# Queries, keys and values of the second layer from seven products of quarters instead of eight, in jobs of half a group

## The chip, the cores and the metric

The kernel runs on one core of one Trainium2 chip. The metric is the device time of one execution in microseconds (us), lower is better. TensorE (PE) multiplies matrices into PSUM; VectorE (DVE), ScalarE (ACT) and GpSimd (POOL) work on vectors; SyncE (SP) issues most of the transfers. Each engine runs its own instructions in the order of the program.

## What is computed

A graph attention layer (first layer) is followed by a self-attention layer (second layer), for 8 batches of 512 tokens with 512 features. All data is float32. Only the second layer is touched by the change:

```python
h = _sln(hidden, w, ...)                       # layer norm, scaled and shifted by the condition
qkv = (h @ Wqkv.T + bqkv).reshape(B, N, num_heads, hd, 3)     # 16 heads of 32
energy = jnp.einsum('bhqd,bhkd->bhqk', q, k)
att = jax.nn.softmax(energy, axis=-1) / D ** 0.5
out = jnp.einsum('bhqk,bhkd->bhqd', att, v)
out = jnp.moveaxis(out, 1, 2).reshape(B, N, D)
out = out @ Wp.T + bp
h1 = out + hidden
h2 = _sln(h1, w, ...)
return h2 + h1
```

## The kernel before

The first layer fills the first third of the span and writes its result to `mid` in DRAM. The second layer then goes through 128 steps, 16 for each batch b (`steps`, L683). A step is one group g of 4 heads and one block c of 128 queries; in this text a step is called by its place `at` (0 to 15) in its batch. All instructions are written out by hand in one loop (`tc.manual_schedule()`, at the end of the function), so each engine's order is the order in the text.

In step n the loop issues, in this order:

- in even steps, `weigh(n-2)` and `weigh(n-1)`: probabilities by values, into PSUM tile `pao` (PE, L731). In the last batch each step weighs one step instead;
- `scores(n+1)`: queries by keys for 4 heads into two PSUM tiles `s` of two banks each (PE, L694), and `tops(n+1)`: the maxima over each pair of heads (DVE, L700). There are just two such tiles, so the next scores wait until the exponentials have read these;
- `turn_probs(n, 0)` and `(n, 1)`: four PE transposes of a head's probabilities into one of 3 PSUM banks (`bank`, pool `ps_g`), and an ACT copy to SBUF (L718, L720);
- `exps(n+1)`: four exponentials on ACT (L706);
- the first half of a group: a group is one 128x512 block of q, k, v or of the output projection, 4 k-blocks added up in one of those 3 banks (class `Group`, L136). Each fp32 matmul is two PE instructions in the trace, so half a group is 4 instructions of 128x512;
- `normalize(n+1, 0)`: a reciprocal on DVE (L711) and two POOL multiplications (L713);
- `turn_probs(n, 2)` and `(n, 3)`, copied by DVE; `normalize(n+1, 1)`; the rest of an output block where one is due (`finish`, L652 to L655: two DVE instructions, one on POOL, one transfer);
- the second half of the group, and what empties it: an ACT activation with bias (q, k), an ACT copy (v), or for the projection a DVE addition to the residual (L644) and the statistics of the norm (L93 to L97);
- smaller items: norm statistics and norm of batch b+2 (L93, L111; steps 11 to 15), the turning of batch b+1 (`turn`, L123/L124: 4 PE transposes and one ACT activation each; steps 0 and 1, for batch 1 steps 0 to 3), the fetch of batch b+2, a bias on POOL (L115).

`group_of` says which group goes with which step: each step of a batch has exactly one. While batch b is attended to, 12 groups make q, k and v (most of them for batch b+1) and 4 project batch b-1. In the last batch, steps 0 and 1 make its last q and k, and 14 half groups of projections (`endings`) go with the other steps; `finish_last` (L656 to L681) makes the last output block with half-width (256-column) matmuls.

Of the kernel before, what the change touches and what calls it, by code (L numbers as in the profile page):

```python
# [9 lines left out]
F32 = mybir.dt.float32  # L10
# [9 lines left out]
P = 128  # L20
C = N // P
# [23 lines left out]
def graph_then_self_attention(ctx: ExitStack, tc: tile.TileContext, x, x_t, near, near_t, labels, w_self_t, wq, wk_t,  # L45
# [30 lines left out]
    feat = ctx.enter_context(tc.tile_pool(name="feat", bufs=3))  # L76
# [11 lines left out]
    XQ, Z, HT, Q, K, V, AO, GATE, STATS = {}, {}, {}, {}, {}, {}, {}, {}, {}  # L88
# [28 lines left out]
    def turn(b, f):  # L117

        if f == 0:
            HT[b] = feat.tile([P, C, N], F32, tag="feat", name=f"ht_{b}")  # L120
        pz = bank(f"pz_{b}_{f}")
        for c in range(C):
            nc.tensor.transpose(pz[:, c * P:(c + 1) * P], Z[b][:, c, f * P:(f + 1) * P], ident)  # L123
        nc.scalar.activation(HT[b][:, f, :], pz, AF.Identity, bias=gates_t[:, 1, f, b:b + 1], scale=gates_t[:, 0, f, b:b + 1])  # L124

    class Group:
# [5 lines left out]
        def half(self, n, take=True):  # L132
            if n == 0:
                self.out = bank(self.name)
            for k in (2 * n, 2 * n + 1):
                nc.tensor.matmul(self.out, self.stationary(k), self.moving(k), start=(k == 0), stop=(k == C - 1))  # L136
            if n == 1 and take:
                self.after(self.out)

    def q_or_k(b, i, f):  # L140
        def after(out):
            at = (HG * b + f) % 5
            dst = (qkp if at else qk0).tile([P, N], F32, tag=f"{'qk'[i]}{at}", name=f"{'qk'[i]}_{b}_{f}")
            nc.scalar.activation(dst, out, AF.Identity, bias=col["b_q" if i == 0 else "b_k"][:, f:f + 1])
            (Q, K)[i][b, f] = dst
        return Group(f"pqk_{b}_{i}_{f}", lambda k: W1[i][:, k, f * P:(f + 1) * P], lambda k: HT[b][:, k, :], after)

    def value(b, c):
        def after(out):
            if c == 0:  # L150
                V[b] = kv.tile([P, C, HM], F32, tag="kv", name=f"v_{b}")[:, :, 0:F]
            nc.scalar.copy(V[b][:, c, :], out)
        return Group(f"pv1_{b}_{c}", lambda k: HT[b][:, k, c * P:(c + 1) * P], lambda k: W1[2][:, k, :], after)


    with ExitStack() as l0:
# [3 lines left out]
        pro = l0.enter_context(tc.tile_pool(name="pro", bufs=1))  # L160
        ps = l0.enter_context(tc.tile_pool(name="ps0", bufs=4, space=PSUM))
# [3 lines left out]
        def bank(name):  # L165
            return ps.tile([P, 512], F32, tag="bank", name=name)
# [113 lines left out]
        def self_feat_main(b, blocks_of_f):  # L280
            if 0 in blocks_of_f:
                SF[b] = feat.tile([P, C, N], F32, tag="feat", name=f"sf_{b}")
            psf = {f: bank(f"psf_{b}_{f}") for f in blocks_of_f}
            for k in range(C):
                for f in blocks_of_f:
                    nc.tensor.matmul(psf[f], ws[:, k, f * P:(f + 1) * P], VT[b][:, k, :], start=(k == 0), stop=(k == C - 1))  # L286
            return psf
# [258 lines left out]
        for n, (b, c) in enumerate(slots):  # L546
# [18 lines left out]
            for i in {26: (0,), 27: (1,), 29: (2,), 30: (3,)}.get(n, ()):  # L565
                group = q_or_k(0, i, 0) if i < 2 else value(0, i - 2)
                group.half(0)
                group.half(1)
# [50 lines left out]
    qkp = ctx.enter_context(tc.tile_pool(name="qkp", bufs=1, reuse_waits="tile"))  # L619
    aop = ctx.enter_context(tc.tile_pool(name="aop", bufs=8, reuse_waits="tile"))  # L620
    gp = ctx.enter_context(tc.tile_pool(name="gp", bufs=2, reuse_waits="tile"))
# [3 lines left out]
    ps_g = ctx.enter_context(tc.tile_pool(name="ps_g1", bufs=3, space=PSUM))  # L625
# [5 lines left out]

    wp = W1[3]
# [3 lines left out]
    bv = w1.tile([P, C], F32, name="bv")  # L636

    def project(b, c):
        def after(out):
            if c == 0:  # L640
                GATE[b] = gp.tile([P, 2, F], F32, tag="gate", name=f"gate_{b}")
                nc.sync.dma_start(GATE[b], gates[b].partition_broadcast(P))
            h1 = XQ[b][:, c, :]
            nc.vector.tensor_tensor(h1, out, h1, ALU.add)  # L644
            statistics(h1, f"h1_{b}_{c}")
        return Group(f"ppj_{b}_{c}", lambda k: AO[b, k][:, c * P:(c + 1) * P], lambda k: wp[:, k, :], after)
# [49 lines left out]
    def tops(n):  # L696
        TOP[n] = small.tile([P, 4], F32, tag="top", name=f"top_{n}")
        DEN[n] = small.tile([P, 4], F32, tag="den", name=f"den_{n}")
        for pair in range(2):
            nc.vector.tensor_reduce(TOP[n][:, 2 * pair:2 * pair + 2], S[n][pair], AX.X, ALU.max, negate=True)  # L700

    def exps(n):
        E[n] = []
        for j in range(4):
            e = ep.tile([P, N], F32, tag="e", name=f"e_{n}_{j}")
            nc.scalar.activation(e, S[n][j // 2][:, j % 2, :], AF.Exp, bias=TOP[n][:, j:j + 1], accum_out=DEN[n][:, j:j + 1])  # L706
            E[n].append(e)
# [7 lines left out]
    def turn_probs(n, j):  # L715
        pt = bank(f"pt1_{n}_{j}")
        for k in range(C):
            nc.tensor.transpose(pt[:, k * P:(k + 1) * P], E[n][j][:, k * P:(k + 1) * P], ident)  # L718
        et = ET[n, j] = tp.tile([P, C, P], F32, tag="et", name=f"et_{n}_{j}")
        (nc.scalar.copy if j < 2 else nc.vector.tensor_copy)(et, pt.rearrange("p (k n) -> p k n", k=C))  # L720

    def weigh(n):
# [10 lines left out]
        if c == (0 if last else C - 1):  # L733
            AO[b, g] = aop.tile([P, N], F32, tag="ao", name=f"ao_{b}_{g}")
# [5 lines left out]
    def group_of(b, at):  # L740

        own = {0: (0, 1), 1: (1, 1), 2: (0, 2), 3: (1, 2), 4: (0, 3), 5: (1, 3)} if b == 0 else {0: (0, 3), 1: (1, 3)}
        if at in own:
            return q_or_k(b, *own[at])
        if b == B - 1:
            return None
        if b > 0 and at in (2, 4, 6, 8):
            return project(b - 1, at // 2 - 1)
        i = at - 6 if b == 0 or at > 8 else (at - 3) // 2
        if i in (2, 3, 4, 5):  # L750
            return value(b + 1, i - 2)
        return q_or_k(b + 1, i % 2, i // 2 if i < 2 else i // 2 - 2)


    endings = [(B - 2, 0), (B - 2, 1), (B - 2, 2), (B - 1, 0), (B - 1, 1), (B - 2, 3), (B - 1, 2)]
    ending = [project(*e) for e in endings]

    with tc.manual_schedule():
        nc.vector.tensor_scalar(bv, col["b_v"], att_scale, None, ALU.mult)
        nc.sync.dma_start(bp_bc, rows[ROW_BP].partition_broadcast(P))  # L760
        fetch(2)
        scores(0)
        tops(0)
        exps(0)
        for c in (2, 3):
            group = value(0, c)
            group.half(0)
            group.half(1)
        for pair in range(2):
            normalize(0, pair)  # L770

        for n, (b, g, c) in enumerate(steps):
            at = n % 16
            group = group_of(b, at)
            more = n + 1 < len(steps)
            if b == B - 1 and at > 0:
                if at > 1:
                    weigh(n - 2)
            elif n > 0 and n % 2 == 0:
                weigh(n - 2)  # L780
                weigh(n - 1)
            if more:
                scores(n + 1)
                tops(n + 1)
            for j in (0, 1):
                turn_probs(n, j)
            if more:
                exps(n + 1)
            if group:
                group.half(0)  # L790
            elif b == B - 1 and more:
                ending[at // 2 - 1].half(at % 2, take=False)
            if more:
                normalize(n + 1, 0)
            for j in (2, 3):
                turn_probs(n, j)
            if more:
                normalize(n + 1, 1)
            if 0 < b < B - 1 and at in (3, 5, 7, 9):
                finish(b - 1, (at - 3) // 2)  # L800
            if b == B - 1 and at > 2 and at % 2 and more:
                ending[at // 2 - 1].after(ending[at // 2 - 1].out)
            if b == B - 1 and at >= 4 and at % 2 == 0:
                finish(*endings[at // 2 - 2])
            if group:
                group.half(1)

            if 11 <= at < 16 and b + 2 < B:
                if at > 11:
                    norm(b + 2, at - 12)  # L810
                if at < 15:
                    norm_stats(b + 2, at - 11)
            if at < (4 if b == 0 else 2) and b + 1 < B:
                for f in (at,) if b == 0 else (2 * at, 2 * at + 1):
                    turn(b + 1, f)
            if at == 9 and b > 0 and b + 2 < B:
                fetch(b + 2)
            first = 0 if b == B - 1 else 10
            if first <= at < first + C:
                bias(b, at - first)  # L820
        ending[-1].half(1)
        weigh(len(steps) - 2)
        weigh(len(steps) - 1)
        finish(*endings[-1])
# [57 lines left out]
```

## Time and profile before

| | |
|---|---|
| runs | 1360.03, 1360.10, 1361.98 us; median 1360.1 us |
| the profiled execution | 1364.07 us, of which 1362.3 us are the span of the trace |
| granted TensorE clock | 0.996 |
| busy, share of the span | PE 99%, DVE 67%, ACT 50%, POOL 51% |
| scores of step 0 of batches 1 to 7 start at | 529.00, 648.32, 767.64, 886.96, 1006.28, 1125.60, 1244.92 us: 119.32 us a batch |
| within a batch, scores to scores | 6.41 us, 8.29 us where `weigh` lies between, alternating; with the turning of the next batch 7.28 and 9.16 |
| last batch | 5.70 to 6.16 us a step from its third step on |

A timeline row gives the start, the length, the engine, the line, the operation with its tiles and how many instructions are merged. A group row gives the line, engine, tiles, shape and count, then the busy time and the mean length of one, and the idle time in front of them with what ended it. PE's matmuls overlap: a row of a matmul is longer than the distance to the next one's start, so distances between starts are used below.

### The profile page before, as it was taken

How to read it: one execution, taken by the hardware profiler on the slowest of the kernel's cores; microseconds unless marked ns; L12 is line 12 of the kernel's file. 1: busy time of each engine (PE TensorE's matmuls, PEld its weight loads, DVE VectorE, ACT ScalarE, POOL GpSimd, SP SyncE). 2: the span in 40 equal slices, each digit the busy share in tenths (PEclk: the TensorE clock that was granted, in tenths of full speed). 3: DMA queues.
4: the chain of work that ended last, by engine and by line, in shares of the span. 5: the costliest groups of instructions: out<-in, count | busy, mean ns of one | idle time of the engine just before them, and what ended most of it. 6: DMA issues, size and time to landing. Idle time of an engine off the chain costs nothing.

```text
span 1362.3 us, 27708 instructions
## 1 busy us (share of the span) xinstructions
PE 1344.2 (99%) x10499; PEld 823.7 (60%) x10499; DVE 907.2 (67%) x1589; ACT 687.5 (50%) x1639; POOL 692.2 (51%) x808
## 2 busy tenths in 40 slices
PE   9999999999989999999999999999999999999997
PEld 6566666666665555555555555555555555555665
DVE  4567677677644556676576667657666765765797
ACT  1322223122225666656665665666566566656664
POOL 0255654465653345455455545545554554554665
PEclk9999999999999999999999999999999999999999
DMA  9614452262221000001001000100100010000010
GB/s 339 205 70 146 138 182 88 92 216 71 88 70 55 2 1 1 9 17 55 1 18 63 2 9 17 55 1 17 63 1 9 17 56 1 17 32 1 9 41 32
DMA packets 46514, 78.53 MB, mean 58 GB/s; under 512 B 9872, under 2 KB 14416, under 8 KB 46384
## 3 DMA queue, kind: packets, MB, share of 16 engines
q1 hardware_dynamic: 45440, 75.57, 16.1%
q8 instruction: 85, 1.39, 0.4%
q0 software_dynamic: 512, 0.66, 0.2%
q10 hardware_dynamic: 432, 0.55, 0.1%
q14 instruction: 45, 0.37, 0.1%
HBM read 59.27 MB, written 17.49 MB: 56 GB/s over the span
## 4 chain that ended last, share of the span: by engine, by line
PE 93%; DVE 4%; POOL 2%; issue 0%; DMA 0%; ACT 0%; POOLq 0%; DVEq 0%; ACTq 0%
PE pt L718 18%; PE pqk L136 16%; PE s L694 10%; PE pao L731 9%; PE pss L457 8%; PE ppj L136 8%; PE pv L136 8%; PE psf L286 7%; PE po L498 2%; PE pw L426 1%; PE ptw L486 1%; PE pz L123 1%; PE pq L407 1%; PE po L496 1%; POOL t L464 1%; POOL t L463 1%
## 5 line engine op out<-in xcount | busy, mean ns | idle before, releaser
L713 POOL TENSOR_SCALAR e<-e,den 128x512 f32<-128x512 f32 x512 | 374.0, 730 | 433.6 <-DVE den L711 383.0
L700 DVE TENSOR_REDUCE top<-s 128x2 f32<-128x1024 f32 x256 | 301.3, 1218 | 196.3 <-PE s L694 196.3
L706 ACT ACTIVATE e<-s,top 128x512 f32<-128x512 f32 x512 | 346.6, 700 | 16.9 <-DVE top L700 16.8
L718 PEld LDWEIGHTS pt<-ident,e 128*128 128x128 f32 x2048 | 229.4, 141 | 165.2 <-issue 89.8
L718 PE MATMUL pt<-ident,e 128*128 128x128 f32 x2048 | 273.1, 276 | 1.0 <-POOL e L713 0.9
L720 ACT COPY et<-pt 128x512 f32<-128x512 f32 x256 | 137.7, 589 | 223.5 <-PE pt L718 223.4
L136 PE MATMUL pqk<-ht,w 128*128 128x512 f32 x512 | 240.6, 593 | 0.0
L720 DVE COPY et<-pt 128x512 f32<-128x512 f32 x256 | 164.2, 683 | 0.9 <-PE pt L718 0.6
L694 PE MATMUL s<-k,q 32*128 32x512 f32 x1024 | 149.8, 641 | 0.0
L457 PE MATMUL pss<-kq,sf 128*128 128x320 f32 x512 | 143.2, 433 | 1.0 <-DVE kq L414 1.0
L731 PEld LDWEIGHTS pao<-et,v 128*32 128x32 f32 x4096 | 107.4, 110 | 42.2 <-issue 41.4
L731 PE MATMUL pao<-et,v 128*32 128x128 f32 x4096 | 126.7, 274 | 0.5 <-ACT ao L736 0.5
L136 PEld LDWEIGHTS pqk<-ht,w 128*128 128x128 f32 x512 | 87.6, 190 | 62.5 <-issue 62.1
L136 PE MATMUL pv<-w,ht 128*128 128x512 f32 x256 | 121.4, 600 | 2.1 <-DVE x L499 2.1
L457 PEld LDWEIGHTS pss<-kq,sf 128*128 128x128 f32 x512 | 94.9, 190 | 37.5 <-ACT sf L293 1.5
L136 PE MATMUL ppj<-w,ao 128*128 128x512 f32 x248 | 116.7, 593 | 0.0
L286 PE MATMUL psf<-vt,ws 128*128 128x512 f32 x256 | 115.0, 592 | 0.0
L706 ACT ACTIVATION_READ_ACCUMULATOR e<-s,top 128x1 f32 x512 | 111.2, 217 | 0.0
L711 DVE RECIPROCAL den<-den 128x2 f32<-128x2 f32 x256 | 42.5, 166 | 85.9 <-ACT e L706 85.9
L480 POOL TENSOR_TENSOR t<-t,den 128x640 f32<-128x640 f32 x32 | 40.7, 1272 | 83.4 <-DVE den L479 82.7
L286 PEld LDWEIGHTS psf<-vt,ws 128*128 128x128 f32 x256 | 48.3, 190 | 50.7 <-issue 46.6
L488 ACT COPY wt<-ptw 128x640 f32<-128x640 f32 x32 | 22.2, 693 | 108.0 <-PE ptw L486 107.6
(197 smaller groups left out, 1375.4 us busy)
## 6 DMA issues: line engine op xcount, KB each, us to landing
x<-in_x SPq DMA_DIRECT2D x8, 1024.0 KB
mid<-x SPq DMA_DIRECT2D x32, 256.0 KB
xq<-mid SPq DMA_DIRECT2D x8, 1024.0 KB
out<-o SPq DMA_DIRECT2D x31, 256.0 KB
vt<-in_x_t SPq DMA_DIRECT2D x7, 1024.0 KB
labels<-in_labels SPq DMA_DIRECT2D x16, 440.0 KB
wq<-in_wq SPq DMA_DIRECT2D x4, 1024.0 KB
gate<-gates SPq DMA_DIRECT2D x8, 512.0 KB
```

The costliest lines, as they stand in the source:

```text
L136: nc.tensor.matmul(self.out, self.stationary(k), self.moving(k), start=(k == 0), stop=(k == C - 1))
L286: nc.tensor.matmul(psf[f], ws[:, k, f * P:(f + 1) * P], VT[b][:, k, :], start=(k == 0), stop=(k == C - 1))
L457: nc.tensor.matmul(o, SF[b][:, k, cut], KQ[b][:, k, on], start=(k == 0), stop=(k == C - 1))
L480: nc.gpsimd.tensor_tensor(tv, tv, den.to_broadcast([P, 2 * H, NG]), ALU.mult)
L694: nc.tensor.matmul(S[n][j // 2][:, j % 2, :], Q[b, g][on, c * P:(c + 1) * P], K[b, g][on, :], start=True, stop=True)
L700: nc.vector.tensor_reduce(TOP[n][:, 2 * pair:2 * pair + 2], S[n][pair], AX.X, ALU.max, negate=True)
L706: nc.scalar.activation(e, S[n][j // 2][:, j % 2, :], AF.Exp, bias=TOP[n][:, j:j + 1], accum_out=DEN[n][:, j:j + 1])
L711: nc.vector.reciprocal(DEN[n][:, at], DEN[n][:, at])
L713: nc.gpsimd.tensor_scalar(E[n][j], E[n][j], DEN[n][:, j:j + 1], att_scale, ALU.mult, ALU.mult)
L718: nc.tensor.transpose(pt[:, k * P:(k + 1) * P], E[n][j][:, k * P:(k + 1) * P], ident)
L720: (nc.scalar.copy if j < 2 else nc.vector.tensor_copy)(et, pt.rearrange("p (k n) -> p k n", k=C))
L731: nc.tensor.matmul(PAO[b, g][DH * j:DH * (j + 1), at], V[b][:, k, DH * h:DH * (h + 1)], ET[n, j][:, k, :], start=(k == 0), stop=(k == C - 1))
```

## The change

Batches 1 to 7 get q, k and v by one level of Strassen's algorithm: the 512x512 weights and the 512x512 turned tokens are cut in quarters, and seven products of quarters take the place of eight. A product (`product`) is 4 matmuls of 256 columns in one PSUM bank; DVE adds it to the one or two quarters of the result that need it, one after another, in place. Sums of weight quarters are made once (DVE, in batch 0: `weight_sums`), sums of token quarters for each batch (POOL: `token_sums`). Batch 0 keeps the ordinary groups (`own` jobs, f = 1 to 3), and one of them is moved in front of the loop.

Work is now handed out in jobs of half a group's size, two places a step (`job(b, 2*at)` and `job(b, 2*at+1)`): a product, half a projection block (256 columns), or half an own group. `JOBS` lists them: batches 1 to 5 have 8 halves of projections and 21 products in 32 places, with the places 1, 3 and 17 empty. All jobs, and the turning of tokens from batch 2 on, share one PSUM bank (`ps_j`, bufs=1); the transposed probabilities have two banks where there were three. The third transposed head of a step is copied by ACT now (in the last batch only in steps with a `finish`), and the exponentials come in pairs: two before the first job, two after the copy of the third head. `finish` moves from the odd steps 3, 5, 7, 9 to the end of the even steps 2, 4, 6, 8; the norm statistics go, two at a time, to the end of steps 10 and 12. Half of the turning ends on DVE.

The diff, cut to what is spoken of:

```diff
-    def turn(b, f):
+    def turn(b, f, psum=None, by_scalar=True):
...
-        nc.scalar.activation(HT[b][:, f, :], pz, AF.Identity, bias=..., scale=...)
+        if by_scalar:
+            nc.scalar.activation(HT[b][:, f, :], pz, AF.Identity, bias=term, scale=factor)
+        else:
+            nc.vector.tensor_scalar(HT[b][:, f, :], pz, factor, term, ALU.mult, ALU.add)
...
-    ps_g = ctx.enter_context(tc.tile_pool(name="ps_g1", bufs=3, space=PSUM))
+    ps_g = ctx.enter_context(tc.tile_pool(name="ps_g1", bufs=2, space=PSUM))
+    ps_j = ctx.enter_context(tc.tile_pool(name="ps_j1", bufs=1, space=PSUM))
...
+    def token_sums(b, n):
...
+        nc.gpsimd.tensor_tensor(SUMS["t", n], x0, x1, ALU.subtract)
...
+    def product(b, i, n):
...
+        out = job_bank(f"pst_{b}_{i}_{n}").rearrange("p (m n) -> p m n", m=2)
+        fixed, moving = (t, a) if i == 2 else (a, t)
+        for m in range(2):
+            for k in range(2):
+                nc.tensor.matmul(out[:, m, :], fixed[:, k, m * P:(m + 1) * P], moving[:, k, :], start=(k == 0), stop=(k == 1))
...
+        if n == 1 and i < 2:
+            nc.vector.tensor_tensor(c_(1, 0), out, bias_2, ALU.add)
+        elif n == 1:
+            nc.vector.tensor_copy(c_(1, 0), out)
+        for dst, src in {2: [((0, 0), (1, 0))], 6: [((1, 0), (1, 0))], 5: [((1, 1), (1, 0))], 3: [((0, 1), (1, 1))],
+                         4: [((1, 0), (1, 0))], 7: [((1, 1), (1, 1)), ((1, 0), (1, 0))]}.get(n, ()):
+            if i < 2 and n in (2, 3):
+                for j in range(2):
+                    nc.vector.scalar_tensor_tensor(c_(*dst)[:, j, :], out[:, j, :], b_less[:, i, j:j + 1], c_(*src)[:, j, :], ALU.add, ALU.add)
+            else:
+                nc.vector.tensor_tensor(c_(*dst), out, c_(*src), ALU.add)
+
+    def project(b, c, n):
...
+        out = job_bank(f"ppj_{b}_{c}_{n}")[:, 0:M]
+        on = slice(n * M, (n + 1) * M)
+        for k in range(C):
+            nc.tensor.matmul(out, AO[b, k][:, c * P:(c + 1) * P], wp[:, k, on], start=(k == 0), stop=(k == C - 1))
+        h1 = XQ[b][:, c, :]
+        nc.vector.tensor_tensor(h1[:, on], out, h1[:, on], ALU.add)
+        if n == 1:
             statistics(h1, f"h1_{b}_{c}")
...
+    keys_and_queries = (made(q, 1, 2, 6, 5) + made(k, 1, 2, 6) + made(q, 3) + made(k, 5, 3)
+                        + made(q, 4, 7) + made(k, 4, 7))
+    JOBS = {0: [("own", i, f, n) for i, f in ((k, 1), (q, 2), (k, 2), (q, 3), (k, 3)) for n in range(2)]
+            + made(v, 1, 2, 6, 5, 3, 7, 4) + [None] + keys_and_queries}
+    for b in range(1, B - 1):
+        pv, pp = made(v, 1, 2, 6, 5, 3, 4, 7), out_of(0, 1, 2, 3)
+        JOBS[b] = [pp[0], None, pp[1], None, pv[0], pp[2], pv[1], pp[3], pv[2], pv[3], pp[4], pv[4], pp[5], pv[5], pp[6], pv[6], pp[7]]
+        if b < B - 2:
+            JOBS[b] += [None] + keys_and_queries
+        else:
+            kq = keys_and_queries
+            JOBS[b][13] = None
+            JOBS[b][15:] = [pp[7], kq[0], kq[1], kq[2], kq[3], None] + kq[4:8] + [None] + kq[8:]
+    LAST = made(v, 4, 7) + [("project", B - 2, 0, 0), None]
...
+        LAST += [("project",) + job, None]
...
+    FINISH = {b: {2: (b - 1, 0), 4: (b - 1, 1), 6: (b - 1, 2), 8: (b - 1, 3)} for b in range(1, B - 1)}
+    FINISH[B - 1] = {3: (B - 2, 0), 5: (B - 2, 1), 7: (B - 2, 2), 9: (B - 1, 0), 12: (B - 1, 1), 13: (B - 2, 3), 15: (B - 1, 2)}
...
             if more:
                 scores(n + 1)
-                tops(n + 1)
+                for pair in range(2):
+                    tops(n + 1, pair)
+            if 0 < b < B - 1 and at < 2:
+                turn(b + 1, 2 * at, job_bank)
             for j in (0, 1):
-                turn_probs(n, j)
+                turn_probs(n, j, nc.scalar.copy)
             if more:
-                exps(n + 1)
-            if group:
-                group.half(0)
...
+                exps(n + 1, 0)
+            job(b, 2 * at)
             if more:
                 normalize(n + 1, 0)
-            for j in (2, 3):
-                turn_probs(n, j)
+            turn_probs(n, 2, nc.vector.tensor_copy if last and (at not in FINISH[b] or not more) else nc.scalar.copy)
+            turn_probs(n, 3, nc.vector.tensor_copy)
+            if more:
+                exps(n + 1, 1)
+            job(b, 2 * at + 1)
             if more:
                 normalize(n + 1, 1)
...
-            if group:
-                group.half(1)
+            if at in FINISH.get(b, ()):
+                finish(*FINISH[b][at])
...
+            if b + 2 < B:
+                for i in {11: (0,), 13: (1,), 14: (2,), 15: (3,)}.get(at, ()):
+                    norm(b + 2, i)
+                for i in {10: (0, 1), 12: (2, 3)}.get(at, ()):
+                    norm_stats(b + 2, i)
...
+            elif at < 2 and b + 1 < B:
+                turn(b + 1, 2 * at + 1, job_bank, by_scalar=False)
...
+                    token_sums(b + 1, i)
+            if b == 0 and at < 12:
+                weight_sums((v, q, k)[at // 4], at % 4)
```

## The prediction

> **What bounds it now.** I read the page's busy shares and chain first.
>
> ```profile
> PE 1344.2 (99%) x10499; PEld 823.7 (60%) x10499; DVE 907.2 (67%) x1589; ACT 687.5 (50%) x1639; POOL 692.2 (51%) x808
> ...
> PE 93%; DVE 4%; POOL 2%; issue 0%; DMA 0%; ACT 0%; POOLq 0%; DVEq 0%; ACTq 0%
> ```
>
> PE is the bound, but its busy time is modelled, so I look for gaps in PE's timeline, here of two steps in mid batch:
>
> ```profile
> 717.14 1.14 PE L694 MATMUL s<-k,q 32*128 32x512 f32 x8
> 718.21 1.09 PE L718 MATMUL pt<-ident,e 128*128 128x128 f32 x8
> 719.14 1.88 PE L136 MATMUL ppj<-w,ao 128*128 128x512 f32 x4
> 720.86 1.04 PE L718 MATMUL pt<-ident,e 128*128 128x128 f32 x8
> 721.73 1.88 PE L136 MATMUL ppj<-w,ao 128*128 128x512 f32 x4
> 723.55 1.14 PE L694 MATMUL s<-k,q 32*128 32x512 f32 x8
> ...
> 729.95 1.30 PE L731 MATMUL pao<-et,v 128*32 128x128 f32 x40
> ```
>
> No gap. From the starts: scores 1.07, two transposes 0.93 or 0.87, half a group 1.72 (4 x 0.429), `weigh` 1.88. Two steps take 14.70 and every batch 119.32. Less PE work is worth its time only while nothing else makes PE wait. The costs of the other engines, by shape:
>
> ```profile
> L700 DVE TENSOR_REDUCE top<-s 128x2 f32<-128x1024 f32 x256 | 301.3, 1218 | 196.3 <-PE s L694 196.3
> L720 DVE COPY et<-pt 128x512 f32<-128x512 f32 x256 | 164.2, 683 | 0.9 <-PE pt L718 0.6 <-DVE den L711 0.3
> L653 DVE SCALAR_TENSOR_TENSOR o<-o,mv_h,xq 128x512 f32<-128x512 f32 x31 | 30.5, 985 | 3.6 <-POOL mv_h L97 0.4
> L652 DVE SCALAR_TENSOR_TENSOR o<-xq,mv_h,gate 128x512 f32<-128x512 f32 x31 | 28.5, 920 | 0.0
> L644 DVE TENSOR_TENSOR xq<-ppj,xq 128x512 f32<-128x512 f32 x31 | 21.3, 688 | 18.6 <-PE ppj L136 18.6
> L668 PE MATMUL ppj_last<-w,ao 128*128 128x256 f32 x16 | 3.7, 386 | 0.0
> ```
>
> The last batch has less PE work a step (5.70), and shows what lies beneath:
>
> ```profile
> 1284.36 0.93 DVE L652 SCALAR_TENSOR_TENSOR o<-xq,mv_h,gate 128x512 f32<-128x512 f32 x1
> 1285.39 0.99 DVE L653 SCALAR_TENSOR_TENSOR o<-o,mv_h,xq 128x512 f32<-128x512 f32 x1
> 1286.31 2.34 DVE L700 TENSOR_REDUCE top<-s 128x2 f32<-128x1024 f32 x2
> ...
> 1287.62 0.69 ACT L706 ACTIVATE e<-s,top 128x512 f32<-128x512 f32 x1 [0.43 <-DVE top L700]
> ...
> 1289.62 0.69 ACT L706 ACTIVATE e<-s,top 128x512 f32<-128x512 f32 x1
> 1289.98 1.60 PE L694 MATMUL s<-k,q 32*128 32x512 f32 x8
> ...
> 1291.51 1.09 PE L718 MATMUL pt<-ident,e 128*128 128x128 f32 x8
> ```
>
> A `finish` (1.95) ahead of the maxima delays them by a microsecond (they start 2.19 after the scores at 1284.12, elsewhere 1.18), the exponentials follow late, and the next scores need 1.53 instead of 1.07, for their second pair waits until the fourth exponential has read its tile. DVE's queue reaches PE.
>
> **PE work.** Starts in the L668 block are 0.216 apart: a job is 8 x 0.216 = 1.73, against 1.72. A batch of 32 half groups (54.9) becomes 29 jobs (50.1): 4.8 less, 7 x 4.8 = 33.6 in all. The Trainium skill (Perfetto Trace Analysis, Optimizing Tensor Performance, Matmuls) holds larger matmuls to be more efficient; the row makes that 0.012 a job, 0.35 a batch.
>
> **DVE, ACT, POOL work.** Each product leaves by DVE. The three-way form on PSUM is not in the trace; the nearest row is L644, 0.69; two half-width corrections cost 0.84 (two of L671, 0.42) to 0.96 (two of L680, 0.48), taken 0.95. Products add (8 + 6 + 6) x 0.69 + 4 x 0.95 = 17.6 a batch, halved projections 4 x (2 x 0.42 - 0.69) = 0.6, turning 2 x 0.69 = 1.4; one copy a step goes to ACT (-16 x 0.68 = -10.9). DVE goes from 82 busy in 120 (the window 650 to 770) to 91: not the bound by its sum, so what decides is its order. ACT gains 16 copies x 0.59 and loses 8 x 0.69 + 4 x 0.59 + 2 x 0.77: even. Token sums (POOL, 4 x 1.27 by L115) lie in POOL's idle 3.4 a step and cost nothing; without it up to 5 a batch. Weight sums on DVE: 0.54 (L111 on `early`) to 0.69, taken 0.65. None of the added operations can gain by itself: they are additions to their queues. No transfer is added; the gate's and the fetch's are issued a step or two earlier on SP, which mostly waits for `finish`. The granted clock should stay: it is 0.99 in the last batch, where PE waits too.
>
> **The order: two steps laid out.** From an even step's scores, by the distances above: first job 2.00, transposes 3.73, second job 4.60, odd scores 6.42; in the odd step, first job 8.42, transposes 10.15, second job 11.02 plus what the even step lost. DVE can empty a job 1.94 after its start (7 x 0.216 + 0.386 + 0.04), and PE follows an emptying after 0.05 (as L731 follows L736 at the end). All jobs share one bank. In steps 2 and 3:
>
> - DVE: maxima 1.18 to 3.53; v1 emptied 3.95 to 4.64, second job at 4.69 (0.09 lost). Copy to 5.6; that job emptied 6.63 to 7.05; reciprocal; `finish` 1.95: free at 9.08.
> - Odd scores stand at 6.5, so the maxima, which could start at 7.7, run 9.08 to 11.43, and v2's emptying ends at 12.12. PE reaches its second job at 11.02 + 0.09 = 11.11 and waits to 12.17: 1.06, with the 0.09 1.15.
> - `weigh` (1.88) then lets DVE catch up before the next even step.
>
> In `before` no such wait is possible: three banks, ACT empties most groups, and `finish` sits in front of `weigh`. By the same layout the seven pairs from 2/3 to 14/15 lose about 1.15, 1.15, 1.05, 0.5, 1.5, 1.8 and 0.8 (two statistics, 2.04, behind steps 10 and 12; a seventh product, 1.38, and a norm, 0.65, behind 14): 8.0 a batch. The skill's same section asks that matmul groups rotate through PSUM banks so that one is emptied while the next runs. By that rule, kept, the waits would be about 0 and the batch 1 shorter than now; with one bank the rows make them 8.0.
>
> **Empty places.** In an even step ACT copies heads 0 and 1 from 1.82 on and runs two exponentials from 2.80 (0.67 apart). Copy 2 waits for its transposes, 3.73 + 0.74 (in the trace, transposes at 703.52, copy at 704.26) = 4.48, and stands before exponentials 3 and 4, which start at 5.02 and 5.69 and end at 6.4; so the second pair of odd scores starts at 6.5 however little PE has to do. An empty second place in an even step thus gains almost nothing: place 17 loses 1.8 of its 1.8; place 1, with the turned tokens' bank waits (0.2 twice) and an ACT activation (0.77) ahead of the copies, loses 1.9 over steps 0 and 1. Only place 3 pays.
>
> **Sum.** Batches 1 to 5: 8.0 + 3.7 - 4.8 = +6.9 each, +34.5. Batch 0: the group moved ahead of the loop +3.4 (PE idles 2.1 there, ended by DVE, not to be filled), place 17 empty for nothing, steps 4 to 15, with weight sums too behind the even ones up to 10, +5.2: +8.6. Batch 6: no norm statistics, three more empty places of which 13 and 25 are second places of even steps: +3.4. Batch 7: steps with `finish` 6.5 and those after 6.2 (copy 2 on ACT), against 5.7 to 6.15: +4; two products for two groups and an earlier last projection -2.5: +1.5. Total +48.0: the profiled 1364.1 (its span 1362.3 and 1.8 around it) would become 1412, and the median, 0.3% below it, 1360.1 + 48.0 = 1408.
>
> **Rivals.**
>
> - *Faster: PE stays the bound* (0.18). DVE is free before 7.7 in odd steps and the exponentials end early enough: then the 33.6 arrive, 1360.1 - 33.6 = 1327, or, with the empty places still lost (6 x 3.7 = 22), 1349. For it: DVE is idle a quarter of the time even then, and `before` shows no wait at all in mid batch. Against: the last batch. It decides at a tail of some 0.6 behind an even step; the tails are 1.95 and 2.04.
> - *Half the waits* (0.25): `finish` without POOL's company takes 1.5 (L652 at 1351.60: 0.74), emptyings are shorter: 4 less a batch, 6 batches, 24: 1384.
> - *Waits as laid out or more* (0.54): 1408; if late exponentials or POOL's sums (5 a batch) bite also in even steps, up to 1425.
> - *It does nothing that counts* (0.03): savings and waits cancel.
>
> Faster by over 0.2% 0.18, within 0.2% (what a measurement can tell from no change) 0.03, slower 0.79. The range, 1350 to 1425, leaves out the full gain and the far end of POOL's delays; without the faster cases it would be 1372 to 1425.
>
> **What would show it.** After: batch length about 126 instead of 119.3; PE's second job in odd steps starts 1 us late, released by DVE's emptying (L728, L721, L741 as releasers of PE); maxima of odd steps following finishes and statistics on DVE; job blocks 1.73 long; scores in steps 0 and 8 stretched by exponentials. I am wrong if odd steps show no such wait (then the layout of DVE fails), or if jobs take over 1.8 (then the price of the half width does).

## The result, and the profile after

| | before | after |
|---|---|---|
| median (range, 4 runs each in the same session) | 1361.04 us (1360.03 to 1362.10) | 1404.7 us (1403.37 to 1406.60) |
| profiled execution, its span | 1364.07, 1362.3 | 1403.37, 1401.3 |
| granted TensorE clock | 0.996 | 0.999 |
| a middle batch, scores to scores | 119.32 | 125.20 |

The ratio is 1.0322 (95% interval 1.0304 to 1.0340): the kernel became 3.2% slower. The forecast was 1408 and slower. The spans of the two profiled executions are not quite comparable: where the second layer begins, PE's clock was halved twice in that of before and never in that of after, which the last section shows.

Busy shares and the chain on the page of after:

```profile
PE 1349.8 (96%) x11251; PEld 974.5 (70%) x11251; DVE 958.7 (68%) x1732; ACT 686.1 (49%) x1653; POOL 733.6 (52%) x836
...
PE 74%; DVE 19%; POOL 2%; ACT 2%; issue 2%; DMA 0%; POOLq 0%; DVEq 0%; ACTq 0%
```

DVE's share of its time hardly moved (67% to 68%), yet its share of the chain that ends last went from 4% to 19%. That pair of numbers is the result in short: DVE did not run out of time, it came to stand in PE's way. Where, PE's timeline of steps 2 and 3 of a middle batch shows (start, length, engine, line, instruction, count; in brackets an idle time and what ended it). From here on a step's scores are those that its place in the loop issues, though they belong to the next step:

```profile
682.02 1.14 PE L791 MATMUL s<-k_pair,q_pair 32*128 32x512 f32 x8
...
684.02 1.89 PE L704 MATMUL pst<-w,ht 128*128 128x256 f32 x8
685.75 1.04 PE L815 MATMUL pt<-ident,e 128*128 128x128 f32 x8
686.70 1.99 PE L739 MATMUL ppj<-w,ao 128*128 128x256 f32 x8
688.63 1.14 PE L791 MATMUL s<-k_pair,q_pair 32*128 32x512 f32 x8
...
690.63 1.89 PE L704 MATMUL pst<-w,ht 128*128 128x256 f32 x8
692.36 1.04 PE L815 MATMUL pt<-ident,e 128*128 128x128 f32 x8
693.89 1.99 PE L739 MATMUL ppj<-w,ao 128*128 128x256 f32 x8 [0.50 <-DVE v L728]
```

In the even step the second job starts 0.95 after its transposes; in the odd step 1.53 after them, released by DVE's L728. L728 is what empties the one job bank. DVE in the same stretch:

```profile
683.20 2.35 DVE L798 TENSOR_REDUCE top<-s 128x2 f32<-128x1024 f32 x2 [1.11 <-PE s L791]
685.96 0.69 DVE L721 COPY v<-pst 128x512 f32<-128x512 f32 x1 [0.40 <-PE pst L704]
...
689.15 0.73 DVE L749 SCALAR_TENSOR_TENSOR o<-xq,mv_h,gate 128x512 f32<-128x512 f32 x1
689.98 0.99 DVE L750 SCALAR_TENSOR_TENSOR o<-o,mv_h,xq 128x512 f32<-128x512 f32 x1
690.90 2.34 DVE L798 TENSOR_REDUCE top<-s 128x2 f32<-128x1024 f32 x2
693.16 0.67 DVE L728 TENSOR_TENSOR v<-pst,v 128x512 f32<-128x512 f32 x1
```

Read it backwards from PE's wait. L728 ends at 693.83, PE goes on at 693.89. L728 stands behind the maxima of 690.90, with no idle time between them. These could have started 1.18 after the odd scores (as in the even step: 683.20 after 682.02), at 689.81, and stood behind the two instructions of `finish` until 690.90. The job itself was ready to be emptied at 690.63 + 1.94 = 692.57. So the `finish` placed at the end of step 2 is what PE waits for in step 3, by way of the maxima and the emptying queued behind it.

The costs of the emptyings are as assumed (group rows, mean ns of one after the bar):

```profile
L741 DVE TENSOR_TENSOR xq<-ppj,xq 128x256 f32<-128x256 f32 x62 | 26.0, 420 | 43.5 <-PE ppj L739 43.5
L728 DVE TENSOR_TENSOR v<-pst,v 128x512 f32<-128x512 f32 x49 | 33.1, 688 | 30.9 <-PE pst L704 30.9
L726 DVE SCALAR_TENSOR_TENSOR q_pair<-pst,b_less,q_pair 128x256 f32<-128x256 f32 x28 | 12.3, 480 | 17.2 <-PE pst L704 17.2
```

Where an empty place saves PE nothing, PE's timeline of steps 8 and 9 shows it:

```profile
733.85 1.13 PE L791 MATMUL s<-k_pair,q_pair 32*128 32x512 f32 x4
735.57 1.13 PE L791 MATMUL s<-k_pair,q_pair 32*128 32x512 f32 x4 [0.58 <-ACT e L803]
```

The scores of step 9 come 4.70 after those of step 8 (at 729.16), since place 17 is empty; but their second pair has to wait for the fourth exponential and starts at +6.41. The transposes, which follow the scores by 1.07 in step 8, start only at 736.62, so 1.70 later than that. The job that was left out would have taken 1.73: the time saved is handed back one step later.

### The profile page after: what moved, and what is told of

It reads as the page before. It is cut to its first block, busy times and chain, and to the rows that moved or that the text cites. A ratio compares the mean times of both kernels' runs of the same rounds, so it can differ in the third digit from the quotient of the medians.

```text
span 1401.3 us, 29426 instructions
## 1 busy us (share of the span) xinstructions
PE 1349.8 (96%) x11251; PEld 974.5 (70%) x11251; DVE 958.7 (68%) x1732; ACT 686.1 (49%) x1653; POOL 733.6 (52%) x836
## 4 chain that ended last, share of the span: by engine, by line
PE 74%; DVE 19%; POOL 2%; ACT 2%; issue 2%; DMA 0%; POOLq 0%; DVEq 0%; ACTq 0%
PE pst L704 16%; PE pt L815 11%; PE pao L828 9%; PE pss L474 8%; DVE top L798 7%; PE s L791 7%; PE psf L303 7%; PE ppj L739 6%; PE pqk L141 2%; PE po L515 2%; DVE o L750 2%; ACT e L803 2%; DVE o L749 1%; DVE st L93 1%; PE pw L443 1%
## 5 line engine op out<-in xcount | busy, mean ns | idle before, releaser
L810 POOL TENSOR_SCALAR e<-e,den 128x512 f32<-128x512 f32 x512 | 380.5, 743 | 353.0 <-DVE den L808 206.6
L817 ACT COPY et<-pt 128x512 f32<-128x512 f32 x374 | 207.6, 587 | 267.1 <-PE pt L815 266.9
L815 PEld LDWEIGHTS pt<-ident,e 128*128 128x128 f32 x2048 | 229.6, 141 | 108.9 <-POOL e L810 55.6
L815 PE MATMUL pt<-ident,e 128*128 128x128 f32 x2048 | 274.8, 276 | 3.0 <-POOL e L810 1.3
L791 PE MATMUL s<-k_pair,q_pair 32*128 32x512 f32 x992 | 163.2, 640 | 5.6 <-ACT e L803 4.7
L739 PE MATMUL ppj<-w,ao 128*128 128x256 f32 x496 | 119.9, 385 | 2.9 <-DVE v L728 2.9
L803 ACT ACTIVATION_READ_ACCUMULATOR e<-s,top 128x1 f32 x512 | 107.4, 210 | 0.0
L739 PEld LDWEIGHTS ppj<-w,ao 128*128 128x128 f32 x496 | 89.5, 190 | 17.6 <-DVE v L728 4.4
L817 DVE COPY et<-pt 128x512 f32<-128x512 f32 x138 | 93.3, 681 | 11.9 <-PE pt L815 7.5
L791 PEld LDWEIGHTS s<-k_pair,q_pair 32*128 32x128 f32 x992 | 46.0, 183 | 50.2 <-ACT e L803 34.3
L97 POOL TENSOR_TENSOR mv_h<-mv_h,minus_half 128x1 f32<-128x1 f32 x31 | 17.0, 547 | 98.0 <-DVE den L808 98.0
L492 ACT ACTIVATE t<-t 128x640 f32<-128x640 f32 x32 | 23.6, 737 | 78.1 <-POOL t L489 78.1
```

Source lines behind the costliest of these rows:

```text
L739: nc.tensor.matmul(out, AO[b, k][:, c * P:(c + 1) * P], wp[:, k, on], start=(k == 0), stop=(k == C - 1))
L791: nc.tensor.matmul(S[n][j // 2][:, j % 2, :], Q[b, g][on, c * P:(c + 1) * P], K[b, g][on, :], start=True, stop=True)
L803: nc.scalar.activation(e, S[n][pair][:, j % 2, :], AF.Exp, bias=TOP[n][:, j:j + 1], accum_out=DEN[n][:, j:j + 1])
L810: nc.gpsimd.tensor_scalar(E[n][j], E[n][j], DEN[n][:, j:j + 1], att_scale, ALU.mult, ALU.mult)
L817: copy(et, pt.rearrange("p (k n) -> p k n", k=C))
```

## Experiments

The theory: PE waits in odd steps because the one job bank is emptied behind work that the change put at the end of even steps (`finish`, statistics); the empty place 17 is lost to the exponentials. The first rival: DVE now simply has too much to do, wherever it stands ("amount"). The second: the waits come from the split and order of other work around them, such as exponentials in pairs, the copy by ACT, or two banks for transposed probabilities; then moving the tails would give little. Each diff is against the changed kernel unless another one is named. "Pairs" are two steps, scores to scores.

### The tails back behind odd steps

```diff
-    FINISH = {b: {2: (b - 1, 0), 4: (b - 1, 1), 6: (b - 1, 2), 8: (b - 1, 3)} for b in range(1, B - 1)}
+    FINISH = {b: {3: (b - 1, 0), 5: (b - 1, 1), 7: (b - 1, 2), 9: (b - 1, 3)} for b in range(1, B - 1)}
...
-                for i in {11: (0,), 13: (1,), 14: (2,), 15: (3,)}.get(at, ()):
+                for i in {12: (0,), 14: (1,), 15: (2, 3)}.get(at, ()):
...
-                for i in {10: (0, 1), 12: (2, 3)}.get(at, ()):
+                for i in {11: (0, 1), 13: (2, 3)}.get(at, ()):
...
-            if at == 8 and b > 0 and b + 2 < B:
+            if at == 9 and b > 0 and b + 2 < B:
```

> The changed kernel, with finish moved back to the ends of odd steps (3, 5, 7, 9), the norm statistics to the ends of steps 11 and 13, the norms to 12, 14, 15 and the fetch to step 9. No work is added or left out. Theory (the order on VectorE: a tail behind an even step makes the odd step's maxima late, the only job bank is emptied late, TensorE waits): the odd intervals of 9.08 to 9.78 us fall to 8.3 to 8.7, a middle batch from 125.2 to about 120.5 us, the whole to about 1376 us. Rival A (VectorE's amount of work is what costs): no change, 1405 us. Rival B (the price is that of half-width matmuls or of the exponentials' new order): no change, 1405 us.

Measured: 1373.0 us (1372.71 to 1375.58, 4 runs), ratio to before 1.0090 (1.0074 to 1.0106); a middle batch 120.02. So 31.7 of the 43.7 us that the change cost come back with nothing but the place of these tails (the norms and the fetch move along with them), at the same amount of DVE work. DVE and PE in the pair that was shown above, first DVE:

```profile
682.61 2.35 DVE L798 TENSOR_REDUCE top<-s 128x2 f32<-128x1024 f32 x2 [0.57 <-PE s L791]
685.36 0.69 DVE L728 TENSOR_TENSOR v<-pst,v 128x512 f32<-128x512 f32 x1 [0.40 <-PE pst L704]
```

Then PE, the end of the odd step:

```profile
685.16 1.04 PE L815 MATMUL pt<-ident,e 128*128 128x128 f32 x8
686.11 1.99 PE L739 MATMUL ppj<-w,ao 128*128 128x256 f32 x8
```

The odd maxima start 1.18 after their scores (681.43), DVE is idle for 0.40 until the product is ready, and the second job follows its transposes by 0.95 as in even steps.

### Only the second maximum made to give way

If it is the queue ahead of the emptying that counts, then it must also help to leave `finish` where the change put it and to take something else out of the way: in odd steps of batches 0 to 6 the second of the two maxima goes behind the emptying of the first job.

```diff
-                for pair in range(2):
-                    tops(n + 1, pair)
+                tops(n + 1, 0)
+                if n % 2 == 0 or last:
+                    tops(n + 1, 1)
...
             job(b, 2 * at)
+            if more and not (n % 2 == 0 or last):
+                tops(n + 1, 1)
```

> The changed kernel, with one edit: in odd steps of batches 0 to 6 the maxima of the second pair of heads stand behind the emptying of the first job instead of in front of it. All tails stay behind the even steps. Theory (the job bank is emptied late because the emptying is queued behind two maxima that start late): with one maximum (1.17 us) less in front, most odd steps lose their wait; a middle batch about 120.6 us, the whole about 1376 us. Rival A (amount of work on VectorE): no change, 1405 us. Rival C (it is the late exponentials, not the late emptying, that hold TensorE): slower than 1405 us, since the second pair of exponentials comes still later.

Measured: 1382.75 us (1381.20 to 1384.26), ratio 1.0158 (1.0140 to 1.0175); a middle batch 121.32. The waits of the odd steps went (pairs 2/3, 4/5 and 6/7 15.09, 14.91 and 14.74, from 15.68, 15.68 and 15.78). What falls short of the expected time is a new wait, in step 1 of each batch:

```profile
677.05 1.06 PE L828 MATMUL pao<-et,v 128*32 128x128 f32 x26 [0.91 <-DVE et L817]
```

There the second maximum comes to stand behind an emptying and the residual's statistics (674.11 to 675.20), so the copy of the fourth head stands behind both and `weigh` waits for it. Pair 0/1 takes 16.12 instead of 14.99. The rule of the queue holds, in both directions; the batch estimate missed by this wait.

### The same amount of DVE work, behind odd or behind even steps

Two statistics of 0.7 us each, whose results nobody uses, are added at the end of three steps of batches 1 to 6: 4.2 us of DVE work a batch in both kernels.

```diff
                 finish(*FINISH[b][at])
+            if 0 < b < B - 1 and at in (5, 7, 9):
+                for i in range(2):
+                    st = small.tile([P, 6], F32, tag="extra", name=f"extra_{n}_{i}")
+                    nc.vector.bn_stats(st, XQ[b][:, i, :])
```

> The changed kernel, with two more norm statistics of a 128x512 block (about 0.7 us each, results unused) on VectorE at the ends of the odd steps 5, 7 and 9 of batches 1 to 6. Theory (order): the odd step's end is covered by the following probabilities-by-values block, so it costs 0 to 0.3 us a batch: 1405 to 1407 us. Rival A (amount of work on VectorE): 4.2 us a batch, 6 batches, +25 us: 1430 us.

Measured: 1404.35 us (1403.45 to 1407.57), ratio 1.0321; a middle batch 125.23, against 125.20 without them. Added DVE work at this place costs nothing.

With `at in (4, 6, 10)` instead:

> The same two extra statistics at the ends of the even steps 4, 6 and 10 of batches 1 to 6. Theory (order): every microsecond there goes to the path, except in step 10 of batch 6, which has no other tail: 3 x 1.4 = 4.2 us a batch, about +24 us: 1428 us. If both places cost the same, amount decides and not order.

Measured: 1434.0 us (1433.02 to 1438.86), ratio 1.0543 (1.0516 to 1.0570). The odd steps behind the three places grew from 9.08, 9.36 and 9.59 to 10.26, 10.55 and 10.78, so by 1.18 each for 1.4 of work; by this the batch is 3.6 longer (the shortest one took 128.79), and batch 6, where the statistics behind step 10 cost nothing, 2.4: 20 over six. Of the rest up to the 31.0 by which the spans differ, 8 are a second effect, told in the last section: after five of these waits PE's clock fell. The remaining 2.5 lie ahead of batch 1 and at the very end, at a halved clock too.

So the amount rival falls: the same work costs nothing or 29 us by its place alone, some 20 of them by waits for DVE alone.

### Place 19 empty instead of 17

Against the kernel with the tails behind odd steps, batches 0 to 5:

```diff
-            + made(v, 1, 2, 6, 5, 3, 7, 4) + [None] + keys_and_queries}
+            + made(v, 1, 2, 6, 5, 3, 7, 4) + keys_and_queries[:2] + [None] + keys_and_queries[2:]}
...
-            JOBS[b] += [None] + keys_and_queries
+            JOBS[b] += keys_and_queries[:2] + [None] + keys_and_queries[2:]
```

> The kernel with the tails behind odd steps (1373.0 us), with one edit: in batches 0 to 5 the empty place moves from 17 (second place of the even step 8) to 19 (second place of the odd step 9), the first two query products moving up. Theory (an empty second place in an even step gains nothing, since the next scores wait for exponentials that stand behind the third copy): steps 8 and 9, now 4.70 + 10.19 us, come to about 6.4 + 6.7 us, 1.7 us less a batch, 6 batches: about 1363 us. Rival (an empty place is worth a job wherever it stands): no change, 1373 us.

Measured: 1363.2 us (1360.89 to 1365.31, 12 runs) against 1361.76 for before on that chip, ratio 1.0006 (0.9996 to 1.0015): level with before. Steps 8 and 9 take 6.43 + 6.58 = 13.01 instead of 4.70 + 10.19 = 14.89. That is the whole 1.73 of the job and 0.15 of wait. An empty second place of an odd step is followed by `weigh` (1.88), during which the exponentials get ahead; that of an even step is followed directly by scores that wait for them.

### The third head copied by DVE in steps 0 and 8

If place 17 is lost because ACT copies the third head ahead of two exponentials, giving that copy to DVE must give time back there. Against the kernel with the tails behind odd steps:

```diff
-            turn_probs(n, 2, nc.vector.tensor_copy if last and (at not in FINISH[b] or not more) else nc.scalar.copy)
+            turn_probs(n, 2, nc.vector.tensor_copy if (0 < b < B - 1 and at in (0, 8)) or last and (at not in FINISH[b] or not more) else nc.scalar.copy)
```

> The kernel with the tails behind odd steps (1373.0 us), with one edit: in steps 0 and 8 of batches 1 to 6 the third transposed head is copied by VectorE, so ScalarE runs its last two exponentials without waiting for it. Theory (it is that copy that holds the next scores): steps 8 and 9 fall from 14.9 to about 14.1 us, steps 0 and 1 from 15.0 to about 14.3 us: 1.4 us a batch in five batches and 0.7 us in batch 6, about -8 us: 1365 us. Rival (VectorE's maxima, or the number of exponentials, hold the scores): no gain, or a loss of up to 0.6 us a step for VectorE's copy: 1373 to 1379 us.

Measured: 1366.98 us (1366.48 to 1369.56), ratio 1.0036 (1.0023 to 1.0049), 6.0 less than without it. Pair 0/1 went from 14.99 to 14.13, as expected. Pair 8/9 went only from 14.89 to 14.73, where some 14.1 were expected. All engines at step 8 to 9:

```profile
725.34 2.06 PE L791 MATMUL s<-k_pair,q_pair 32*128 32x512 f32 x8
...
725.98 0.15 DVE L96 TENSOR_SCALAR mv_h<-mv_h 128x1 f32<-128x1 f32 x1
...
726.05 0.15 DVE L808 RECIPROCAL den<-den 128x2 f32<-128x2 f32 x1
...
726.22 0.55 POOL L97 TENSOR_TENSOR mv_h<-mv_h,minus_half 128x1 f32<-128x1 f32 x1 [2.33 <-DVE den L808]
...
726.86 3.05 POOL L810 TENSOR_SCALAR e<-e,den 128x512 f32<-128x512 f32 x4
...
727.61 1.44 PE L815 MATMUL pt<-ident,e 128*128 128x128 f32 x8 [0.20 <-POOL e L810]
```

The exponentials are earlier, but the next in line takes over: the first reciprocal stands on DVE behind the statistics of the projected block (ending with L96), on POOL the last operation of these statistics (L97) stands ahead of the multiplications, which start only at 726.86, and the transposes (L815) wait for POOL. So in step 8 ACT's copy was one of two limits, nearly equally late.

### A kernel with these lessons together

Against the kernel with the tails behind odd steps: place 19 empty in batches 0 to 5; in batch 6 the places 15, 19 and 27 beside 1 and 3; in steps 2 to 7 a half projection always first (its emptying is 0.42) and a product of the values second; the third copy by DVE in step 0 and in the whole last batch.

```diff
-        pv, pp = made(v, 1, 2, 6, 5, 3, 4, 7), out_of(0, 1, 2, 3)
-        JOBS[b] = [pp[0], None, pp[1], None, pv[0], pp[2], pv[1], pp[3], pv[2], pv[3], pp[4], pv[4], pp[5], pv[5], pp[6], pv[6], pp[7]]
+        v7, v4 = made(v, 7, 4)
+        pv, pp = made(v, 1, 2, 6, 5, 3), out_of(0, 1, 2, 3)
+        kq = keys_and_queries
+        JOBS[b] = [pp[0], None, pp[1], None, pp[2], pv[0], pp[3], pv[1], pp[4], pv[2], pp[5], pv[3], pp[6], pv[4], pp[7]]
         if b < B - 2:
-            JOBS[b] += [None] + keys_and_queries
+            JOBS[b] += [v7, v4, kq[0], kq[1], None] + kq[2:]
         else:
-
-            kq = keys_and_queries
-            JOBS[b][13] = None
-            JOBS[b][15:] = [pp[7], kq[0], kq[1], kq[2], kq[3], None] + kq[4:8] + [None] + kq[8:]
+            JOBS[b] += [None] + kq[:3] + [None] + kq[3:8] + kq[8:10] + [None] + kq[10:]
...
-            turn_probs(n, 2, nc.vector.tensor_copy if last and (at not in FINISH[b] or not more) else nc.scalar.copy)
+            turn_probs(n, 2, nc.vector.tensor_copy if last or (b > 0 and at == 0) else nc.scalar.copy)
```

> All products kept, and everything that the runs point to put together: tails behind odd steps, empty places in second places of odd steps (3 and 19; in batch 6 also 15 and 27) except place 1, projection halves as first jobs of steps 2 to 7 (their emptying, 0.42 us, is over before the second job), the third copy by VectorE in step 0 and in the whole last batch. Theory: a middle batch 117 to 117.5 us against 119.3 before, batch 0 about 3 us longer than before (a group moved ahead of the loop), the last batch about 1 us shorter: 1348 to 1353 us, faster than the kernel before (1361 us) by about 0.8%. Rival (the products cannot pay on this kernel, whatever the order): not below 1361 us.

Measured: 1351.5 us (1348.32 to 1352.25, 5 runs) against 1361.76, ratio 0.9915 (0.9899 to 0.9931): faster than both kernels, than before by 0.85%; a middle batch 116.93. Against the kernel with place 19 empty a middle batch is 1.2 shorter, batch 6, with its empty places moved, 5.5, and the last batch 2.3. Its busy shares, then PE at the end of step 3 of a middle batch:

```profile
PE 1325.0 (98%) x11251; PEld 969.4 (72%) x11251; DVE 974.6 (72%) x1744; ACT 680.7 (51%) x1641; POOL 734.7 (55%) x836
```

And PE:

```profile
678.23 1.89 PE L739 MATMUL ppj<-w,ao 128*128 128x256 f32 x8
679.96 1.04 PE L815 MATMUL pt<-ident,e 128*128 128x128 f32 x8
680.84 1.89 PE L704 MATMUL pst<-w,ht 128*128 128x256 f32 x8
682.66 1.95 PE L828 MATMUL pao<-et,v 128*32 128x128 f32 x64
```

The second job follows its transposes by 0.88 (0.87 in before). DVE has 974.6 us of work, more than in the changed kernel (958.7) and 67 more than before, at a shorter time than either.

The pairs of a middle batch, in us; the column "laid out" is the pair of before with the loss that the prediction gave it (for 0/1 and 8/9 with the empty places):

| steps | before | laid out | after | tails odd | and place 19 | all together |
|---|---|---|---|---|---|---|
| 0/1 | 16.44 | 14.9 | 14.99 | 14.99 | 14.99 | 14.13 |
| 2/3 | 14.70 | 15.85 | 15.68 | 15.08 | 15.09 | 14.74 |
| 4/5 | 14.70 | 15.85 | 15.68 | 14.92 | 14.91 | 14.74 |
| 6/7 | 14.70 | 15.75 | 15.78 | 14.74 | 14.74 | 14.74 |
| 8/9 | 14.70 | 15.2 | 15.27 | 14.88 | 13.01 | 13.18 |
| 10/11 | 14.70 | 16.2 | 16.20 | 15.08 | 15.08 | 15.08 |
| 12/13 | 14.70 | 16.5 | 16.38 | 15.09 | 15.09 | 15.09 |
| 14/15 | 14.70 | 15.5 | 15.24 | 15.24 | 15.24 | 15.24 |

## Why the prediction was right, and where its terms were off

- **A job is 1.73.** Right: 684.02 to 685.75 in the timeline. The products did take their time off PE, and the measured loss is what stood against it.
- **The waits in odd steps.** Right in place, releaser and cause, pair by pair (table). The maxima of step 3 were laid out at 9.08 after the even scores and came at 8.88; PE's second job at 12.17 and came at 11.87. Over the seven pairs from 2/3 on, the layout has 8.0 and the trace 7.3. What was mis-sized is `finish`: taken as 1.95, it lasted 1.75 (689.15 to 690.90), because its first instruction took 0.73 where before's row had 0.92. The "half the waits" rival took 1.5 for it, from a first instruction of 0.74 said to be without POOL's company; in the trace POOL was at work for 0.58 of those 0.74. The first instruction did get so short here, with POOL at work for 0.48 of it (it took 0.97 to 1.03 where POOL was at work for 0.88 or more), but the second, with POOL at work for 0.90, stayed at 0.99. The waits were nine tenths of those laid out, not half: 1384 fell.
- **A term that was missing.** A job that finds its bank still being emptied costs 0.10 more than the wait itself: from its start to the next instruction's it takes 1.92 or 1.93 (686.70 to 688.63, 693.89 to 695.82) instead of 1.82. This is why even steps take 6.60 where a full-width product (0.69) goes first and 6.43 where a half projection (0.42) does, and why pairs 2/3 to 6/7 fall to 14.74 in the last kernel. The layout had 0.09 for the wait and nothing for this.
- **Empty places 1 and 17.** Right: the second pair of step 9's scores was laid out at 6.5 and came at 6.41, and moving the empty place to 19 gave 1.88 a batch. That ACT's copy alone stood behind it is only half right: with the copy on DVE, step 0 gained 0.86, but step 8 only 0.16, where POOL, behind a reciprocal and the last operation of the statistics, was as late.
- **Batches 1 to 5.** Laid out +6.9 each, measured +5.9 (125.20): 0.6 of the difference are smaller waits, and 0.35, the width of the jobs, is counted apart in the layout but is already in the measured pairs.
- **Batch 0.** Laid out +8.6. The two profiled executions give +6.0 (129.52 against 123.51), and for the first interval, with the group moved ahead of the loop, 1.3 (12.48 to 13.75) where 3.4 were laid out. But PE's clock was halved twice there in that of before, and not in that of after. The kernel with the third head copied by DVE is the same as the changed one up to its loop, and its trace has two such half-clock stretches too (last section): there the interval is 15.84, so 3.4 more than before, as laid out. With it batch 0 takes +8.1.
- **Batches 6 and 7.** Laid out +3.4 and +1.5; measured +3.05 and +2.3. From its fourth step on the last batch's steps took 6.08 to 6.55, where 6.5 with a `finish` and 6.2 after it were laid out; its remaining 0.8 was not followed further.
- **The sum.** By the spans it is +39.0, where +48.0 were laid out. The two half-clock stretches cost 3.9 (the scores of the loop's first step come at 421.36 with them and at 417.42 without), so at a like clock it is about +42.9, an estimate that the +43.7 of the medians bears out. The difference to 48.0 is 5 less from batches 1 to 5, 0.5 from batch 0, 0.35 from batch 6, and 0.8 more in batch 7. So the size is off by a tenth, for the most part by the waits and the width of the jobs in batches 1 to 5. A small part of the agreement with 1408 is luck: the sum was added to a median of 1360.1, while the median of all four runs of before is 1361.0.
- **The faster rival.** It was said to decide at a tail of some 0.6 behind an even step. The tails were 1.75 and more, so it fell; and when they were moved (and with them the empty places), PE did become the bound again (89% of the chain that ended last, DVE 7%, in the last kernel) and the products paid.
- **DVE's amount.** From 82 busy to 91 a batch was laid out, 8.7 more. The group rows of a middle batch sum to 8.4 more; the busy time rose by 6.0 (81.7 to 87.7), as overlapping starts and ends are counted once. That this load decides nothing by itself is what the two kernels with added statistics showed.

That the products are worth their cost is shown only for the last kernel: 119.32 to 116.93 a batch, of the 4.8 that they take off PE. A better order alone is hardly what did it, since PE's timeline of before shows no gap in mid batch that an order could close; it was not tried by itself. By the table, the rest lies in pairs 10/11 to 14/15 (1.3 over 14.70) and in pair 0/1 (14.13, where 16.44 less two jobs would be 12.98). What a second job bank would do was not tried; the one there is was taken from the transposed probabilities, which now have two banks instead of three.

## What to carry to other kernels

Work taken off the engine that bounds a kernel is worth its time only if what replaces it doesn't make that engine wait: where one buffer takes all results, ask for each use what stands ahead of its emptying in the other engine's queue, and lay out the two together over one period. Side work of an engine with over a quarter of its time free still has a right and a wrong place; it belongs ahead of a long block of the bounding engine that doesn't need the buffer (here `weigh`, 1.88), and by that the same 1.4 us of work cost nothing or 1.18. A gap is best put where the next instruction is not itself waiting for another chain, and after each such wait is removed the next one has to be looked for, since it may be nearly as late.

## What the hardware showed beyond that

**A weight load that is no longer hidden.** PE's weight loads in step 3 of the changed kernel, the job that doesn't wait and the one that does:

```profile
690.52 1.60 PEld L704 LDWEIGHTS pst<-w,ht 128*128 128x128 f32 x8
...
693.89 1.59 PEld L739 LDWEIGHTS ppj<-w,ao 128*128 128x128 f32 x8 [0.74 <-DVE v L728]
```

The first load of the job that isn't held up starts 0.11 ahead of its matmuls (690.63), during the transposes before it. The one that is held up starts with them (693.89 both). This fits the 0.10 that such a job takes longer; that the load is the cause was read from these starts and not tried by itself.

**The clock after a wait.** With the added statistics behind even steps, PE stood idle for 1.98 us in the middle of the kernel, and in some places what followed it was slow. PE's timeline at such a place, then two stretches, one behind the other (from and to, length, then busy time of PE, PEld, DVE, ACT and POOL with counts, granted clock, DMA share, GB/s):

```profile
600.76 1.04 PE L815 MATMUL pt<-ident,e 128*128 128x128 f32 x8
603.78 2.50 PE L704 MATMUL pst<-w,t 128*128 128x256 f32 x8 [1.98 <-DVE xq L741]
606.21 3.06 PE L828 MATMUL pao<-et,v 128*32 128x128 f32 x64
```

```profile
601.71:605.12 3.41, 1.44 (x7) 1.22 (x7) 2.77 (x5) 2.77 (x8) 1.00 (x3) 1.00 0.20 77
605.12:608.54 3.42, 3.42 (x48) 2.55 (x50) 1.36 (x3) 0.51 (x2) 1.23 (x2) 0.50 0.02 5
```

The job took 2.50 instead of 1.99 and `weigh` 3.06 instead of 1.95, so the wait of 2 us cost some 1.6 more. The granted clock was 0.50 for 3.41 us and 1.00 on both sides. In batches 1 to 6 of this run there are five such half-clock stretches of 3.41 us, starting at 605.12, 639.26, 768.96, 1028.38 and 1158.08. From one start to the next it is 10, 38, 76 and 38 times 3.413, so they lie on a fixed grid that does not follow the steps. The run has ten waits of 1.97 to 2.21 us there. The five that lie within one piece of the grid were followed by a halved clock; the five that lie across an edge between two pieces were not (in the closest case, 896.67 to 898.88, 0.22 of the wait lies behind the edge).

The Trainium skill (TensorE: Matmul & The Clock Gate, Part 1: The HAM clock gate) says that the clock is halved after a window of about 3.4 us without activity, and that this window runs freely. The length and the free running agree with these starts. "Without activity" does not: in the pieces ahead of the five half-clock stretches PE was at work for 1.20 to 1.44 us (1.44 in the row above). So here the measurement decides: a wait of 2 us was enough where it fell into one piece. How little work is too little does not come out of this trace: a piece with 1.42 (895.25 to 898.67) was followed by the full clock, and one with 1.82 near the end by a halved one (from 1417.49 on).

The same effect sets single executions of one program apart. First before, where its second layer begins; then the kernel with the third head copied by DVE, which has two half-clock stretches as well, at 402.94 and 409.77:

```profile
403.06:406.47 3.41, 3.41 (x14) 2.72 (x18) 1.23 (x6) 0.00 (x0) 0.65 (x2) 0.50 0.11 37
...
409.89:413.30 3.41, 3.41 (x6) 1.35 (x5) 2.23 (x5) 1.24 (x4) 0.98 (x2) 0.50 0.37 126
```

```profile
417.83 3.60 PE L141 MATMUL pqk<-ht,w 128*128 128x512 f32 x8
421.36 1.14 PE L791 MATMUL s<-k,q 32*128 32x512 f32 x8
```

In before the loop's first scores start at 417.97; the 421.36 here are 3.4 later, by the group moved ahead of the loop (3.53, from 417.83 on). The other kernels share this stretch with the changed one: without a halved clock there, the interval ahead of these scores is 13.74 or 13.75 (three kernels), with one half-clock stretch, starting between 407.15 and 408.17, it is 15.44 (four kernels), and with two 15.84. So the spans of two profiled executions can be compared only after the granted clock of both has been looked at, piece by piece.
